# Block-wise turning of attention probabilities on VectorE with row-tiled context products, and a bitwise search for the top-k thresholds on ScalarE

## The chip, the core and the metric

The kernel runs on one core of one Trainium2 chip. The core has five instruction streams that run independently and meet through semaphores: TensorE (PE; its weight loads are shown apart as PEld), VectorE (DVE), ScalarE (ACT), GpSimd (POOL) and SyncE (SP), which issues most transfers. Each stream executes its instructions in the order in which the built program has them. The metric is device time of one execution in microseconds (us).

## What is computed

Four batches of 512 tokens with 512 features pass through two blocks. The parts that matter here:

```
# block 0, attention over contexts h (512 x 128 per batch)
sim       = einsum(Q, K) / (sqrt(32) * 4)             # 512 x 512
threshold = top_k(sim, 153)[..., -1:]                 # 153rd largest value of each row
A         = sigmoid(sim) * (sim >= threshold)
adj       = (A + A.T) * 0.5
x         = x + tanh(g) * ((1 - gamma) * layernorm(x) + gamma * adj)
# block 0, feed-forward: Hadamard rotations, 8-bit rows, ternary weights (feed0)
# block 1, attention with 16 heads over the rotated contexts kv_r (512 x 128)
scores    = einsum(q_r, k_r)                          # 16 heads, 512 x 512
attn      = softmax(scores)
ctx_c     = attn @ kv_r                               # per head, 512 x 128
x         = x + tanh(g) * (ctx_c projected by each head's 128 x 512 matrix, summed)
# block 1, feed-forward with normalized rows and ternary weights (feed1)
```

All products of the two attentions are in float32.

## The kernel before

**Order of the work.** Batch 0 passes alone through block 0 (`adjacency(0)`, `feed0(0)`), while `ahead` prepares what all batches need: the rotated contexts `kv`, one 128 x 512 output matrix per head (`om`, kept in DRAM), and the keys. Then `attention` (L917) walks through 4 x 8 pairs of heads. Each pair has four steps, one for each 128 rows j of queries. In a step `scores(j)` makes the score products of both heads, and the *next* pair's preparation is put in (`head`: query projections pqh; `rope`: products pb and rotation; `rotated`: product pr). After each step a planner (L1029) adds background work: `before(b)` for batches 1 to 3, which is the block-0 work of the next batch (`adjacency`, `keys`, `feed0`), and for the last batch `last_weights`, which makes block 1's ternary weights and runs `feed1` of batches 0 to 2. Each background generator yields a cost, and a job's costs (230 for a batch, 260 for the last) are spread over its steps. `feed1` of batch 3 ends the kernel. The framework places the instructions at build time in the streams of the engines, by priority and by its own estimate of when they are free; `tc.high_priority` moves instructions ahead, a negative offset moves them back.

**One pair of heads.** `scores(j)`: two products pss (L863, L866), each with 64 rows of the contraction in its own half of the array; VectorE finds the row maximum nm (L871), ACT makes the exponential pp with the row sum (L874) and scales it by the reciprocal (L877). `turn(j)` (L880), two steps behind the scores: TensorE transposes the four 128 x 128 blocks of pp through the identity into ppt (L885), ACT copies ppt to pT (L886). `attended` (L888), when all four tiles are turned: for each head four products of 128 contexts each accumulate pc (L893), and ACT copies it to cxo (L898). `added` (L901): four output products po of two heads each (L905), and VectorE adds them to the tokens x (L910). The heads' `om` are loaded at the start of the pair.

**The top-k threshold.** `adjacency(b)` (L447) takes two row tiles at a time. ACT copies the similarities to sim (L477). Twenty rounds follow: VectorE's MAX8 finds the eight largest of each row (L486), and MATCH_REPLACE overwrites them with a very low number (L491); the 153rd value falls out of the last round. These 20 rounds stand for each of the 16 row tiles of the four batches, put back in priority:

```
for r in range(rounds):
    with tc.high_priority(offset=-FILL):
        for j in pair:
            nc.vector.max(m8[j], cur[j])
    yield 1.3
    with tc.high_priority(offset=-FILL):
        if r < rounds - 1:
            for j in pair:
                nc.vector.match_replace(works[j], m8[j], cur[j], GONE)
    yield 1.4
```

Then a sigmoid on ACT (L496) and one VectorE operation (L497) make the masked values, and L512 to L524 symmetrize them and add them to x.

**Memory.** PSUM has eight banks: four for products (`ps`, tag mm), two for transposes (`pst`, tag tr) and two for background work (`psb`). pT has two buffers of 128 x 2048, one per head.

## Time and profile before

| | |
|---|---|
| three runs, median (lowest to highest) | 2048.83 us (2048.23 to 2052.68) |
| profiled execution, span | 2048.8 us |
| PE busy | 1819.6 us, 89% |
| DVE busy | 1630.3 us, 80% |
| ACT busy | 1081.8 us, 53% |
| POOL busy | 336.1 us, 16% |
| first and last score products (L863) start at | 286.3 and 1914.3 us |
| mean granted TensorE clock | 0.96 of full speed |

The profile is one execution. A line of the groups gives the source line, engine, operation, what is written and read, shapes and count; after the first bar the busy time of the group in us and the mean length of one in ns; after the second the idle time of the engine just before these instructions and what ended it. A float32 product appears as two passes in the counts of PE and PEld. A line of the timeline begins with start and length in us. A line of a stretch gives from, to and length, then for PE, PEld, DVE, ACT and POOL the busy us (and instructions), then the granted clock, the share of the DMA engines and GB/s.

### The profile page before, as it was taken

The page shows a single profiled execution, that of the slowest core. Times are in us where ns is not written, and L with a number is a line of the kernel's source. Part 1 is how long each engine was busy: PE and PEld are TensorE (multiplying, and loading weights), DVE is VectorE, ACT ScalarE, POOL GpSimd, SP SyncE. Part 2 cuts the span into 40 slices and gives each one's busy share as a digit, 9 for nine tenths or more (in the row PEclk, how much of TensorE's full clock was granted, in tenths as well). Part 3 has the DMA queues.
Part 4 walks back from the last instruction along what each step waited for, and adds up shares of the span by engine and source line. Part 5 has one row for each costly group of instructions (what it writes and reads, how often), then busy time and mean ns, then how long its engine had stood idle before and what let it go on. Part 6 is the DMA issues. An engine that isn't in the chain of part 4 may idle for free. (4 is left out here: it accounts for less than half of the span.)

```text
span 2048.8 us, 22947 instructions
## 1 busy us (share of the span) xinstructions
PE 1819.6 (89%) x7874; PEld 889.2 (43%) x7874; DVE 1630.3 (80%) x3305; ACT 1081.8 (53%) x1833; POOL 336.1 (16%) x316
## 2 busy tenths in 40 slices
PE   1268799999999999999999999999989999999898
PEld 0035534436554344455444444555443444444333
DVE  7989699987776999977778999778758556866785
ACT  6935454354434455453444564534786565555544
POOL 3020031123011122130111221301111210111000
PEclk6579899999999999999999999999999999999999
DMA  7451021111111222111122121111783112222011
GB/s 269 155 179 38 1 74 45 55 49 28 42 43 48 89 71 72 38 38 37 41 55 84 57 84 47 35 35 38 241 302 128 50 40 74 68 53 67 21 34 39
DMA packets 115556, 151.90 MB, mean 74 GB/s; under 512 B 57456, under 2 KB 68080, under 8 KB 112368
## 3 DMA queue, kind: packets, MB, share of 16 engines
q1 hardware_dynamic: 109968, 134.51, 22.0%
q0 software_dynamic: 4320, 14.16, 1.9%
q10 hardware_dynamic: 1152, 1.77, 0.2%
q8 instruction: 62, 1.02, 0.2%
q14 instruction: 54, 0.44, 0.1%
HBM read 117.90 MB, written 19.92 MB: 67 GB/s over the span
## 5 line engine op out<-in xcount | busy, mean ns | idle before, releaser
L833 POOL TENSOR_TENSOR ro<-ro,rs 128x512 f32<-128x512 f32 x192 | 255.4, 1333 | 1153.3 <-DVE rs L829 648.3
L874 ACT ACTIVATE pp<-pss,nm 128x512 f32<-128x512 f32 x256 | 174.6, 685 | 272.3 <-DVE nm L871 271.5
L804 PE MATMUL pqh<-hT,wq 128*128 128x512 f32 x512 | 239.7, 606 | 6.8 <-ACT pp L874 5.6
L893 PE MATMUL pc<-pT,kv 128*128 128x512 f32 x512 | 236.0, 600 | 2.7 <-ACT pT L886 2.6
L905 PE MATMUL po<-om,cxo 128*128 128x512 f32 x512 | 229.9, 597 | 0.0
L819 PE MATMUL pb<-qh,wc 128*128 128x512 f32 x384 | 189.4, 613 | 13.6 <-ACT qh L809 7.7
L486 DVE MAX8 m<-work 128x8 f32<-128x512 f32 x304 | 198.7, 684 | 0.6
L871 DVE TENSOR_REDUCE nm<-pss 128x1 f32<-128x512 f32 x256 | 167.8, 683 | 38.1 <-PE pss L866 37.9
L491 DVE MATCH_REPLACE8 work<-m,work 128x512 f32<-128x512 f32 x288 | 193.6, 678 | 0.1
L877 ACT ACTIVATE pp<-pp,rsm 128x512 f32<-128x512 f32 x256 | 178.6, 720 | 27.4 <-DVE rsm L876 26.2
L886 ACT COPY pT<-ppt 128x512 f32<-128x512 f32 x256 | 142.1, 588 | 38.5 <-PE ppt L885 38.0
L885 PEld LDWEIGHTS ppt<-ident,pp 128*128 128x128 f32 x1024 | 117.7, 142 | 96.6 <-issue 37.1
L885 PE MATMUL ppt<-ident,pp 128*128 128x128 f32 x1024 | 147.8, 279 | 10.1 <-ACT pp L877 4.4
L910 DVE SCALAR_TENSOR_TENSOR x<-po,gt,x 128x512 f32<-128x512 f32 x128 | 94.8, 745 | 68.4 <-PE po L905 67.6
L804 PEld LDWEIGHTS pqh<-hT,wq 128*128 128x128 f32 x512 | 93.1, 191 | 128.4 <-issue 89.6
L863 PE MATMUL pss<-kr,qr 64*128 64x512 f32 x256 | 143.4, 641 | 4.4 <-ACT pp L874 2.6
L905 PEld LDWEIGHTS po<-om,cxo 128*128 128x128 f32 x512 | 93.9, 190 | 119.5 <-issue 101.2
L866 PE MATMUL pss<-kr,qr 64*128 64x512 f32 x256 | 143.4, 641 | 0.7 <-DVE ro L827 0.5
L827 DVE TENSOR_TENSOR ro<-pb,cos_q 128x512 f32<-128x512 f32 x192 | 130.9, 682 | 10.3 <-PE pb L819 9.5
L893 PEld LDWEIGHTS pc<-pT,kv 128*128 128x128 f32 x512 | 91.9, 190 | 105.0 <-issue 90.4
L819 PEld LDWEIGHTS pb<-qh,wc 128*128 128x128 f32 x384 | 65.6, 189 | 113.6 <-issue 40.9
L898 ACT COPY cxo<-pc 128x512 f32<-128x512 f32 x64 | 37.4, 584 | 145.1 <-PE pc L893 144.8
(279 smaller groups left out, 3062.0 us busy)
## 6 DMA issues: line engine op xcount, KB each, us to landing
wq<-in_wqh SPq DMA_DIRECT2D x64, 256.0 KB, 2.7
om<-omd SPq DMA_DIRECT2D x64, 256.0 KB, 2.8
wc<-in_wkcq SPq DMA_DIRECT2D x32, 384.0 KB, 3.1
krd<-krs POOLq DMA_DIRECT2D x32, 256.0 KB, 2.5
kr<-krd SPq DMA_DIRECT2D x32, 256.0 KB, 2.7
sa_w1v<-in_gvT SPq DMA_DIRECT2D x8, 1024.0 KB, 5.3
sb_w1v<-in_gvT SPq DMA_DIRECT2D x8, 1024.0 KB, 5.2
wr<-in_wqr SPq DMA_DIRECT2D x32, 192.0 KB, 2.4
```

The costliest lines, as they stand in the source:

```text
L486: nc.vector.max(m8[j], cur[j])
L491: nc.vector.match_replace(works[j], m8[j], cur[j], GONE)
L804: nc.tensor.matmul(pq, self.wqs[i][:, c, :], hT[self.b][:, c, :], start=(c == 0), stop=(c == NC - 1),)
L819: nc.tensor.matmul(pb, self.wc[:, at : at + P], self.qhs[i if i < 2 else o], start=True, stop=True)
L833: nc.gpsimd.tensor_tensor(ro, ro, rs, ALU.add)
L863: nc.tensor.matmul(*args, start=True, stop=True)
L871: nc.vector.tensor_reduce(nm, pss[i], AX.X, ALU.max, negate=True)
L874: nc.scalar.activation(pp, pss[i], AF.Exp, bias=nm, accum_out=sm)
L877: nc.scalar.activation(pp, pp, AF.Copy, scale=rs)
L885: nc.tensor.transpose(pt[:, l, :], pp[:, l * P : (l + 1) * P], ident)
L893: nc.tensor.matmul(pc, kv[self.b][:, l, :], self.pT[i][:, l, :], start=(l == 0), stop=(l == NT - 1),)
L905: nc.tensor.matmul(po, self.cxo[i][:, j * P : (j + 1) * P], self.oms[i], start=(i == 0), stop=(i == 1),)
```

## The change

There are two changes, and what follows from them.

1. **Turning and context product.** `turn(j)` no longer uses TensorE and ACT: VectorE transposes each 128 x 512 tile of probabilities in blocks of 32 x 32, and writes pT. What was at (row 32a + r, context 32c + s) is then at partition 32a + s, column 32c + r: the contexts of one block lie over 32 partitions, and the four groups of 32 partitions hold the four groups of query rows. So `attended` makes 64 products per pair, each with 32 rows of contraction, for context block c and row group g: 32 contexts (kvrep, partitions 32g to 32g + 31) times 256 query rows of both heads. The four groups accumulate in four banks, and ACT copies four pieces to cxo. The contexts have to lie in each of the four groups, so `kvrep` (8 KB per partition) is loaded four times from DRAM for each batch, by `values(b)`; `ahead` writes the rotated contexts to DRAM, and `keys` reads them back. A pair's context and output products now come in the first step of the next pair, behind its first scores and the next query projection. `turn(j)` comes in the step of its scores. The heads' `om` are loaded in that first step as well, behind the previous pair's output products. pT has one buffer for both heads.
2. **Thresholds of batches 1 to 3.** Instead of 20 rounds on VectorE a search finds the threshold bit by bit for all four row tiles at once: ACT counts with Sign and its accumulator how many values of a row lie above a test value (four passes over 128 x 512), and VectorE sets or clears a bit by three operations on 128 x 4. One count for the sign and 31 for the bits follow each other; each needs the previous one's result. Batch 0 keeps the rounds. The tokens x are loaded behind the search.
3. PSUM: the two transpose banks join the products' (six of one kind). The scratch tiles for the start (cxo, pT) are taken from other rings.

The core of the diff:

```diff
-    ps = ctx.enter_context(tc.tile_pool(name="ps", bufs=4, space=bass.MemoryType.PSUM))
-    pst = ctx.enter_context(tc.tile_pool(name="pst", bufs=2, space=bass.MemoryType.PSUM))
+    ps = ctx.enter_context(tc.tile_pool(name="ps", bufs=6, space=bass.MemoryType.PSUM))
...
+    def kth(b, sims):
+        st = small.tile([P, 8, NT], F32, tag="kth", name=f"kth_{b}", bufs=1)
+        cnt, sig, need, test, r, u, hi, lo = (st[:, k, :] for k in range(8))
+        ints = lambda t: t.bitcast(I32)
+        junk = gate_t(f"signs_{b}")
+
+        def signs(**how):
+            for j in range(NT):
+                col = slice(j, j + 1)
+                nc.scalar.activation(
+                    junk, sims[:, j, :], AF.Sign, accum_out=cnt[:, col],
+                    **{k: v[:, col] for k, v in how.items()},
+                )
...
+        for bit in range(30, -1, -1):
+            signs(scale=sig, bias=test)
+            nc.vector.tensor_tensor(ints(r), cnt, need, ALU.is_lt)
+            if bit:
+                nc.vector.tensor_scalar(
+                    ints(r), ints(r), bit, 1 << (bit - 1), ALU.logical_shift_left, ALU.bitwise_or
+                )
+            nc.vector.tensor_tensor(ints(test), ints(test), ints(r), ALU.bitwise_xor)
+            yield 3.4
...
+        for j in range(NT):
+            nc.vector.tensor_scalar(
+                junk, sims[:, j, :], hi[:, j : j + 1], 0.0, ALU.is_ge, ALU.add,
+                accum_out=cnt[:, j : j + 1],
+            )
+        nc.vector.tensor_scalar(ints(u), cnt, float(TOPK), None, ALU.is_ge)
+        nc.vector.copy_predicated(lo, ints(u), hi)
+        yield 5.0
+        return lo
...
+        if not alone[0]:
+            for j in range(NT):
+                psim = bg_ps(f"psim_{b}_{j}")
+                nc.tensor.matmul(psim, qT[:, j * P : (j + 1) * P], kT, start=True, stop=True)
+                nc.scalar.activation(adj[:, j, :], psim, AF.Copy, scale=SIM_SCALE)
+                yield 1.0
+            limit = yield from kth(b, adj)
+            tokens()
+            for j in range(NT):
+                sg = front_t(f"sig_{b}_{j}")
+                nc.scalar.activation(sg, adj[:, j, :], AF.Sigmoid)
+                nc.vector.scalar_tensor_tensor(
+                    adj[:, j, :], adj[:, j, :], limit[:, j : j + 1], sg, ALU.is_ge, ALU.mult
+                )
+        for two in range(0, NT if alone[0] else 0, 2):
...
+    def values(b):
+        t = const.tile([P, 16, DC], F32, tag="kvrep", name=f"kvrep_{b}")
+        rows = kv_d[b].rearrange("(a i) j d -> i j a d", i=32)
+        for g in range(4):
+            nc.sync.dma_start(
+                t[32 * g : 32 * g + 32].rearrange("i (j a) d -> i j a d", j=NT), rows
+            )
+        kv[b] = t
...
         def turn(self, j):
+            if self.pT is None:
+                self.pT = wp.tile([P, 2, NT, S], F32, tag="pT", name=f"pT_{self.u}", bufs=1)
             for i in range(2):
-                pt = tr_ps(f"ppt_{self.u}_{i}_{j}")
-                pp = self.pps.pop((i, j))
-                for l in range(NT):
-                    nc.tensor.transpose(pt[:, l, :], pp[:, l * P : (l + 1) * P], ident)
-                nc.scalar.copy(self.pT[i][:, :, j * P : (j + 1) * P], pt)
+                nc.vector.transpose(self.pT[:, i, j, :], self.pps.pop((i, j)))
 
         def attended(self):
-            self.cxo = []
-            for i in range(2):
-                pc = mm_ps(f"pc_{self.u}_{i}")
-                for l in range(NT):
-                    nc.tensor.matmul(
-                        pc, kv[self.b][:, l, :], self.pT[i][:, l, :],
-                        start=(l == 0), stop=(l == NT - 1),
-                    )
-                cxo = wp.tile([P, S], F32, tag="cxo", name=f"cxo_{self.u}_{i}", bufs=3)
-                nc.scalar.copy(cxo, pc)
-                self.cxo.append(cxo)
+            pcs = [mm_ps(f"pc_{self.u}_{g}") for g in range(4)]
+            for c in range(16):
+                for g in range(4):
+                    rows = slice(32 * g, 32 * g + 32)
+                    with tc.high_priority() if c + g else nullcontext():
+                        nc.tensor.matmul(
+                            pcs[g][:, : 8 * 32], kv[self.b][rows, c, :],
+                            self.pT[rows, :, :, 32 * c : 32 * c + 32].rearrange("p i j s -> p (i j) s"),
+                            start=(c == 0), stop=(c == 15), skip_group_check=True,
+                        )
+            self.cxo = wp.tile([P, 8, 4, 32], F32, tag="cxo2", name=f"cxo_{self.u}", bufs=1)
+            for g in range(4):
+                nc.scalar.copy(self.cxo[:, :, g, :], pcs[g][:, : 8 * 32].rearrange("p (m s) -> p m s", m=8))
...
         for at, (b, g) in enumerate(order):
             nxt = begin(*order[at + 1]) if at + 1 < len(order) else None
-            cur.oms = out_weights(b, g)
             for j in range(NT):
                 cur.scores(j)
...
-                if j > 1:
-                    cur.turn(j - 2)
+                if j == 0:
+                    if prev:
+                        ended(prev)
+                    cur.oms = out_weights(b, g)
+                cur.turn(j)
                 yield b, g
-            cur.turn(NT - 2)
-            cur.turn(NT - 1)
             if nxt:
                 nxt.rotated()
-            cur.attended()
-            cur.added()
```

`ended(p)` is `p.attended()`, `p.added()` and, for the last pair of a batch, the spills of x that stood at the end of the loop, then `values(b + 1)`.

## The prediction

> **What bounds the kernel now.** I read the page's busy table first (PE 89%, DVE 80%, ACT 53%), then busy time by stretches between score products of chosen pairs, then the costliest groups, last single stretches of the timeline. The stretches (us; PE, PEld, DVE, ACT, POOL busy; clock, DMA share, GB/s):
>
> ```profile
> 286.00:406.00 120.00, 115.19 (x362) 48.99 (x362) 117.67 (x262) 56.35 (x116) 23.42 (x19) 1.00 0.16 48
> 406.00:655.00 249.00, 232.83 (x1277) 126.86 (x1276) 195.26 (x352) 114.19 (x210) 43.88 (x42) 0.99 0.17 44
> 655.00:789.00 134.00, 127.95 (x403) 55.35 (x402) 123.31 (x279) 68.02 (x134) 25.61 (x23) 1.00 0.23 71
> ...
> 1485.00:1907.00 422.00, 399.31 (x1399) 175.31 (x1400) 280.91 (x548) 253.80 (x407) 63.14 (x48) 0.99 0.32 95
> ```
>
> From the first score product (286.3) to the last (1914) TensorE is busy about 95% of every stretch: it sets the length. ACT has more than half of each stretch free. The price rows:
>
> ```profile
> L486 DVE MAX8 m<-work 128x8 f32<-128x512 f32 x304 | 198.7, 684 | 0.6
> L893 PE MATMUL pc<-pT,kv 128*128 128x512 f32 x512 | 236.0, 600 | 2.7 <-ACT pT L886 2.6
> ...
> L491 DVE MATCH_REPLACE8 work<-m,work 128x512 f32<-128x512 f32 x288 | 193.6, 678 | 0.1
> ...
> L886 ACT COPY pT<-ppt 128x512 f32<-128x512 f32 x256 | 142.1, 588 | 38.5 <-PE ppt L885 38.0
> ...
> L885 PE MATMUL ppt<-ident,pp 128*128 128x128 f32 x1024 | 147.8, 279 | 10.1 <-ACT pp L877 4.4
> ```
>
> Two heads' scores, the one pair of row tiles in the kernel (start, duration):
>
> ```profile
> 1619.29 0.69 PE L863 MATMUL pss<-kr,qr 64*128 64x512 f32 x1
> ...
> 1619.30 0.69 PE L866 MATMUL pss<-kr,qr 64*128 64x512 f32 x1
> ...
> 1619.83 0.59 PE L863 MATMUL pss<-kr,qr 64*128 64x512 f32 x1
> 1619.83 0.59 PE L866 MATMUL pss<-kr,qr 64*128 64x512 f32 x1
> ```
>
> The two tiles run side by side, pass by pass. And ACT early in the kernel: an accumulating pass that must wait for the previous one, then a pass with per-row scale and bias:
>
> ```profile
> 29.56 1.89 ACT L239 ACTIVATE ja_w0g<-sa_w0g 128x2048 bf16<-128x2048 f32 x1
> 31.36 0.18 ACT L239 ACTIVATION_READ_ACCUMULATOR ja_w0g<-sa_w0g 128x1 f32 x1
> 31.58 1.91 ACT L239 ACTIVATE ja_w0u<-sa_w0u 128x2048 bf16<-128x2048 f32 x1
> ...
> 51.38 0.19 ACT L239 ACTIVATION_READ_ACCUMULATOR ja_w0u<-sa_w0u 128x1 f32 x1
> 51.48 0.80 ACT L514 ACTIVATE x<-x,ckm,ckr 128x512 f32<-128x512 f32 x1
> 52.18 1.90 ACT L239 ACTIVATE ja_w0u<-sa_w0u 128x2048 bf16<-128x2048 f32 x1
> ```
>
> **The change, engine by engine.** The sum goes against the profiled execution: its span of 2048.8 is the median of the three runs (2048.83) to 0.03 us, so I use one number for both.
>
> *TensorE, transposes.* 1024 transposes go. In the timeline eight take 0.87 to 1.04 us from start to start of what follows, so 0.12 each: -120 us, 3.7 per pair of heads (the 147.8 busy counts overlapping tails).
>
> *TensorE, context.* Now a pair takes 7.06 us (16 passes of 0.43). After, 64 products of 256 columns, two passes of half of 0.43 each: 0.43 us a product. Four tiles side by side give 16 x 0.43 = 6.9, all in line 27.5. Two row tiles side by side are in the trace, four are not; I take 6.9 and keep 27.5. But the tiles are not dealt evenly: in the built program's order 12 of the 32 pairs begin like 0,1,0,2,1,3,2,1,3,2 and leave 8 to 14 products of one tile for the end, which nothing accompanies. Walking each pair's order with 0.43 per product and in-order start gives 301 us against 32 x 7.06 = 226: +75. TensorE nets -120 + 75 = -45 us.
>
> The Trainium skill, "TensorE: Matmul & The Clock Gate", section "Part 3: Packing small matmuls", speaks against a full factor of four: it gives 3.07 for four row tiles. By it an even pair would take 27.5 / 3.07 = 9.0 us, an estimate, and the 23 pairs outside the searches would add some 23 x 2 = 47 us to the sum below; no run here shows that figure.
>
> *VectorE.* Gone: 240 MAX8 (0.68), 228 MATCH_REPLACE (0.68) with their loads (0.08): 337 us. New: 256 block transposes; no such row; nearest are 128x512 passes from 0.54 (L184) up to 1.22 for a 1024 wide one (L588); I take 0.68: 174. Some 320 operations on 128x4 at 0.16 to 0.25: 65; twelve 128x512 counts: 8. Net -90, and it stays below TensorE in each stage. The transposes of tile 0 stand in VectorE's line behind the previous pair's context product, as pT has one buffer: VectorE idles there for the product (7 to 12 us). In pairs where it has 50 to 57 us of work beside TensorE's 53 to 57 that shows; I put 8 us per non-search stage.
>
> *ACT.* Gone: 256 copies of 0.59 (142 us). New: 384 counts (3 batches x 32 x 4). Scale and bias by row make 0.80 long, 0.70 start to start (L514 above, against 0.62 for the plain L496); the accumulator read adds 0.10. All counts write one scratch tile, so each waits for the one before: above, a pass into the same scratch starts 0.22 after the accumulator read (31.36 to 31.58), one that is free of it 0.10 after (51.38 to 51.48): +0.12. That is 0.80 without and 0.92 with the wait; lower bound 0.68, the exponential's step. I take 0.90: 346 us. Between bits ACT needs three dependent VectorE operations (0.24 each where such a chain stands, as 229.91, 230.15 at L192 and L194) and two hand-overs of under 0.1: 0.85. In the built order a bit's first count follows the last bit's count directly 59 times.
>
> *Where these counts stand.* This decides. They are not spread over a batch: 109 of batch 1's lie in pairs 0 to 2, all 128 of batch 2's in the first three pairs of their stage, batch 3 the same, most of them in a pair's first step. A typical first step on ACT: two exponentials, two scalings, qh, 18 counts, context copy, count, two copies, 6 counts, copy, 9 counts: 3.2 + 34 x 0.9 + 4 x 0.35 + 8 x 0.85 = 42 us. TensorE's part of that step is 1.1 + 3.6 + 7 to 12 + 7 = 19 to 24 us, and its output product, then the next scores, stand behind the four copies, so behind 25 counts. TensorE waits.
>
> ACT per search stage, from its busy time in the stretch. Batch 1 (286 to 406): 56.4 - 14.1 (24 copies) + 0.7 (context in four pieces) + 98 + 14 (bit waits) = 155, TensorE 103. Batches 2 and 3 (655 to 789, 1069 to 1203): 68 - 14.1 + 0.7 + 115 + 17 + 8 (six more table loads of 1.28) + 3 (two sigmoids, four yb copies moved in) = 198, TensorE 139.
>
> *Elsewhere* TensorE decides. I sum its row prices pair by pair. A plain pair before: pqh 7.3, pb 5.7, pss 4.2, pr 2.7, ppt 3.7, pc 7.1, po 7.0, in all 37.7; the trace has 39.9 from scores to scores, and over all pairs a factor of 1.065 (small waits) gives 1623 for the 1628 us between first and last scores. After, with the uneven tiles, TensorE comes to 218, 260, 260 and 428 in the four stages outside the searches. Stages, before and after: pairs 0 to 2, 120 and 155; 3 to 6, 249 and 228; 7 to 9, 134 and 198; 10 to 14, 280 and 268; 15 to 17, 134 and 198; 18 to 22, 282 and 268; 23 to 31, 428 and 440 (uneven tiles eat the transposes' gain there, and pair 23 has 60 us of ACT work, most of it weight passes ahead of its context copies, against TensorE's 51). Sum 1628 and 1755: +127.
>
> *Costed at nothing.* kvrep, four loads of 256 KB a batch on SP's queue behind the spills and ahead of om: the 256 KB wq lands in 2.7 us, and its first use is a pair (40 us) later; without that cover some 10 us a batch. The context and output products of a pair, with their spills, now follow the next pair's first scores, and om's loads follow them on SP's queue; om is used a pair later. kvd and kvl: one round trip per batch, with pairs to spare. Larger rings for oms and krs at the start: at most the 10 us that pO waits for oms, taken as 0.
>
> Forecast 2048.8 + 127 = **2175 us**.
>
> **Rivals.**
> 1. *ACT keeps up, TensorE decides (faster).* Place: the three search stages. For it: ACT is half idle there (56 of 120). They would take TensorE's 103, 139 and 139, with the others at their sums without my 8s: 1560, so 1985 us. The point: outside the searches I expect -36, so they may take 388 + 36 = 424 us; ACT's other work there is 57 + 83 + 83 = 223; 365 counts must fit in 201, 0.55 us each. Rows say 0.80 at least, and no row with an accumulator is under 0.68.
> 2. *Four tiles do not run side by side (much slower).* 27.5 instead of 7 to 13 per pair: the searches mostly hide it under ACT, the other pairs add about 19 each: some 2600. Against: the L863 and L866 starts, 10 ns apart.
> 3. *The searches cost as said, but less:* counts at 0.80 and bit waits hidden behind exponentials: 25 to 30 less per search stage, and no 8s: 2065. It has my forecast's mechanism at its lower bounds; upper bounds, transposes at 1.22 in VectorE's fullest pairs (+30), uneven tiles and a clock that drops while TensorE waits (0.62 in 0 to 100 us, +25), end at 2255.
>
> **How the numbers follow.** Searches bound by ACT (forecast with rival 3's lower end): 0.78, nearly all of it slower, 2045 to 2260. TensorE decides: 0.15, 1985 to 2045. Tiles in line: 0.05. Unchanged by balance: 0.02. The range 2045 to 2260 leaves out most of the second and all of the third, 2 in 10. A measurement of this kernel tells about 0.2% (4 us) from no change: faster 0.14, same 0.03, slower 0.83.
>
> **What would show it.** Right: in the three search stages ACT busy over 80% and TensorE under 75%, its longest waits at po for cxo and at pss or pqh for the exponentials; counts 0.9 apart; four pc products starting within 0.1 us of each other, ends of some pairs with one tile alone for 3 to 6 us; other stages 10 to 20 us shorter. Wrong: counts under 0.6 apart; TensorE over 90% in the searches; pc taking over 20 us in each pair; VectorE the releaser TensorE waits for longest.

## The result and the profile after

The changed kernel takes 2491.9 us (median of four runs, 2488.1 to 2493.4) against 2050.8 us (2048.2 to 2053.5) for the kernel before in the same job: 1.215 times as long, 95% interval 1.213 to 1.217, so +441 us where +126 was forecast. The direction was right; the time lies above the range, whose upper end was 2260. The profiled execution has a span of 2491.6 us.

The engines' busy line and the row of granted clocks on the page of the changed kernel:

```profile
PE 1885.5 (76%) x10434; PEld 993.9 (40%) x10434; DVE 1563.8 (63%) x3213; ACT 1317.0 (53%) x2433; POOL 330.1 (13%) x320
...
PEclk6658997799998877999887788999877899999899
```

No engine is near full any more. TensorE's share falls from 89% to 76%: it stands still for 606 us (span less busy time) where it stood for 229. Its mean granted clock falls from 0.960 to 0.860. Next the stretches that answer to those of before (us; busy time of PE, PEld, DVE, ACT, POOL; clock, DMA share, GB/s): pairs 0 to 2, 3 to 6, 7 to 9, and 23 to the last score.

```profile
322.60:492.30 169.70, 113.69 (x458) 53.22 (x458) 78.55 (x203) 142.96 (x315) 22.81 (x18) 0.80 0.11 33
492.30:747.30 255.00, 219.42 (x1550) 129.16 (x1550) 191.63 (x350) 100.43 (x193) 43.62 (x43) 0.92 0.15 43
747.30:987.80 240.50, 154.34 (x692) 76.71 (x692) 105.58 (x283) 174.83 (x383) 25.47 (x23) 0.79 0.16 46
...
1839.50:2359.00 519.50, 440.39 (x2252) 215.12 (x2252) 339.02 (x672) 258.57 (x402) 62.85 (x48) 0.90 0.31 96
```

In the search stages ACT is busy 84%, then 73% (174.83 of 240.50), TensorE 67 and 64%: one waits for the other in turn. Where nothing is searched TensorE falls short as well, 86% and 85%, and those stretches were to become shorter.

Every stage (first score of a pair to first score of another; "head" is up to the first score), with four of the experiments told below; the forecast's stages stand beside, the last one as its 440 to the last scores and the 135 that follow them in before:

| us | before | forecast | after | e1 | e2 | e9 | e10 |
|---|---|---|---|---|---|---|---|
| head | 286.3 | 286 | 322.6 | 320.5 | 285.9 | 319.3 | 320.6 |
| pairs 0-2, search | 119.9 | 155 | 169.7 | 158.2 | 139.7 | 151.0 | 146.7 |
| 3-6 | 248.9 | 228 | 255.0 | 252.1 | 262.8 | 235.5 | 242.5 |
| 7-9, search | 134.1 | 198 | 240.5 | 204.9 | 149.3 | 215.2 | 170.8 |
| 10-14 | 280.1 | 268 | 305.5 | 287.3 | 293.9 | 285.7 | 274.0 |
| 15-17, search | 133.9 | 198 | 239.0 | 204.2 | 159.2 | 188.7 | 170.0 |
| 18-22 | 282.1 | 268 | 307.2 | 287.5 | 300.2 | 285.6 | 272.4 |
| 23 to the end | 563.5 | 575 | 652.1 | 643.7 | 577.0 | 616.5 | 581.6 |
| span | 2048.8 | 2175 | 2491.6 | 2358.4 | 2168.0 | 2297.5 | 2178.6 |

The stages are named after the changed kernel, whose counts end with pairs 2, 9 and 17 but for five in pair 3. In the other columns part of the search runs on into the stage that follows: in e2 pairs 7 to 11 hold 28, 29, 30, 27 and 14 of the counts on record, in the changed kernel pairs 7 to 9 hold 50, 40 and 38.

**What TensorE waits for.** From the waits of TensorE in the changed kernel (us in total, times, longest):

```profile
PE po L996 <- ACT cxo L989: 160.4, 17, 21.5
PE pr L882 <- POOL ro L925: 142.3, 37, 9.9
PE pd_f L439 <- DMA zT_f<-q_f: 41.5, 5, 10.6
```

The kernel before had no wait of po for the copies on its list, and of the other two

```profile
PE pr L790 <- POOL ro L833: 10.0, 13, 1.3
...
PE pd_f L436 <- DMA zT_f<-q_f: 6.5, 7, 1.5
```

The first was forecast, the other two were not. The third stands mostly where a batch's preparation ends. The first two can be seen in one search pair (pair 8, 68.9 us; before 42.4). ACT's rows in its first step:

```profile
862.80 0.81 ACT L464 ACTIVATE signs<-adj,kth 128x512 f32<-128x512 f32 x1
863.52 0.19 ACT L464 ACTIVATION_READ_ACCUMULATOR signs<-adj,kth 128x1 f32 x1
863.74 0.81 ACT L464 ACTIVATE signs<-adj,kth 128x512 f32<-128x512 f32 x1
864.46 0.18 ACT L464 ACTIVATION_READ_ACCUMULATOR signs<-adj,kth 128x1 f32 x1
865.33 0.81 ACT L464 ACTIVATE signs<-adj,kth 128x512 f32<-128x512 f32 x1 [0.69 <-DVE kth L482]
...
884.99 0.35 ACT L989 COPY cxo<-pc 128x256 f32<-128x256 f32 x1
```

A count starts 0.94 us after the one before it and 1.59 after a bit's last one, so a bit costs 4.41 us (4.45 by the forecast's 0.90 and 0.85). The fourth context copy stands behind all counts up to 884.99. TensorE in the same pair:

```profile
855.88 13.87 PE L982 MATMUL pc<-pT,kvrep 32*128 32x256 f32 x128
885.39 9.76 PE L996 MATMUL po<-om,cxo 128*128 128x512 f32 x16 [15.63 <-ACT cxo L989]
...
908.81 0.64 PE L882 MATMUL pr<-ro,wr 128*64 128x512 f32 x1
...
915.63 1.12 PE L882 MATMUL pr<-ro,wr 128*64 128x512 f32 x1 [5.75 <-POOL ro L925]
```

The context product was done at 869.7; po could start 15.6 us later and runs 9.76 us instead of the 7.1 that it took before (below). At the pair's end pr waits 5.75 us and its next pass takes 1.12 instead of 0.64. In the changed kernel's pair 26, after a shorter wait, it does not:

```profile
2079.59 0.64 PE L882 MATMUL pr<-ro,wr 128*64 128x512 f32 x1 [1.20 <-POOL ro L925]
```

How the pair's end looked before (pair 26, one with no search):

```profile
1641.07 0.64 PE L790 MATMUL pr<-ro,wr 128*64 128x512 f32 x1
...
1642.74 1.04 PE L885 MATMUL ppt<-ident,pp 128*128 128x128 f32 x8
1643.71 0.64 PE L790 MATMUL pr<-ro,wr 128*64 128x512 f32 x1
...
1644.72 7.13 PE L893 MATMUL pc<-pT,kv 128*128 128x512 f32 x16
1651.69 7.12 PE L905 MATMUL po<-om,cxo 128*128 128x512 f32 x16
```

Transposes lie between the parts of pr, and the last rotated tiles come in time. The context and output products follow the last part of pr here, so they covered nothing of that chain; they lie ahead of it in pairs with much other work (pair 5: 12 of 16 passes of pc).

The rows of what was added:

```profile
L464 ACT ACTIVATE signs<-adj,kth 128x512 f32<-128x512 f32 x372 | 302.0, 812 | 90.6 <-DVE kth L482 82.3
L982 PE MATMUL pc<-pT,kvrep 32*128 32x256 f32 x4096 | 307.2, 380 | 0.0
...
L974 DVE STREAM_TRANSPOSE pT<-pp 128x512 f32<-128x512 f32 x256 | 169.3, 691 | 125.0 <-PE pc L982 119.1
```

These sizes are close to the forecast's (0.80, 301 us, 0.68). What failed is not these prices but what TensorE waits for.

### The profile page after: what moved, and what is told of

Its sections match the earlier page's. It is cut to its first block, busy times and chain, and to the rows that moved or that the text cites. A ratio compares the mean times of both kernels' runs of the same rounds, so it can differ in the third digit from the quotient of the medians.

```text
span 2491.6 us, 28671 instructions
## 1 busy us (share of the span) xinstructions
PE 1885.5 (76%) x10434; PEld 993.9 (40%) x10434; DVE 1563.8 (63%) x3213; ACT 1317.0 (53%) x2433; POOL 330.1 (13%) x320
## 4 chain that ended last, share of the span: by engine, by line
PE 45%; DVE 25%; ACT 21%; DMA 4%; issue 3%; POOL 1%; SPq 0%; ACTq 0%; POOLq 0%; DVEq 0%
ACT signs L464 10%; PE po L996 10%; PE pqh L896 7%; PE pc L982 6%; PE pss L953 3%; DVE rs L924 3%; DVE nm L961 2%; PE pd_f L439 2%; DVE ro L919 2%; PE pzh_f L679 2%; ACT pp L964 2%; PE pb L911 2%; PE pr L882 2%; DVE pT L974 2%; PE pd_g L439 1%
## 5 line engine op out<-in xcount | busy, mean ns | idle before, releaser
L996 PE MATMUL po<-om,cxo 128*128 128x512 f32 x512 | 258.7, 661 | 160.5 <-ACT cxo L989 160.4
L464 ACT ACTIVATE signs<-adj,kth 128x512 f32<-128x512 f32 x372 | 302.0, 812 | 90.6 <-DVE kth L482 82.3
L982 PE MATMUL pc<-pT,kvrep 32*128 32x256 f32 x4096 | 307.2, 380 | 0.0
L982 PEld LDWEIGHTS pc<-pT,kvrep 32*128 32x128 f32 x4096 | 272.8, 185 | 42.5 <-issue 13.7
L896 PE MATMUL pqh<-hT,wq 128*128 128x512 f32 x512 | 257.2, 643 | 2.5 <-ACT hT L854 2.5
L974 DVE STREAM_TRANSPOSE pT<-pp 128x512 f32<-128x512 f32 x256 | 169.3, 691 | 125.0 <-PE pc L982 119.1
L882 PE MATMUL pr<-ro,wr 128*64 128x512 f32 x192 | 120.3, 731 | 142.6 <-POOL ro L925 142.3
L953 PE MATMUL pss<-kr,qr 64*128 64x512 f32 x256 | 162.3, 717 | 16.3 <-ACT qr L942 16.2
L956 PE MATMUL pss<-kr,qr 64*128 64x512 f32 x256 | 162.3, 718 | 0.0
L477 DVE TENSOR_TENSOR kth<-kth 128x4 int32<-128x4 f32 x93 | 17.1, 183 | 226.3 <-ACT signs L464 225.8
L884 PE MATMUL pr<-ro,wr 128*64 128x512 f32 x192 | 120.3, 731 | 0.0
L989 ACT COPY cxo<-pc 128x256 f32<-128x256 f32 x128 | 40.5, 375 | 139.7 <-PE pc L982 139.7
```

The lines of the kernel that those rows point to most:

```text
L464: nc.scalar.activation(junk, sims[:, j, :], AF.Sign, accum_out=cnt[:, col], **{k: v[:, col] for k, v in how.items()},)
L896: nc.tensor.matmul(pq, self.wqs[i][:, c, :], hT[self.b][:, c, :], start=(c == 0), stop=(c == NC - 1),)
L953: nc.tensor.matmul(*args, start=True, stop=True)
L974: nc.vector.transpose(self.pT[:, i, j, :], self.pps.pop((i, j)))
L982: nc.tensor.matmul(pcs[g][:, : 8 * 32], kv[self.b][rows, c, :], self.pT[rows, :, :, 32 * c : 32 * c + 32].rearrange("p i j s -> p (i j) s" ...
L996: nc.tensor.matmul(po, cxo[:, NT * i + j, :], self.oms[i], start=(i == 0), stop=(i == 1))
```

## The experiments

Times are medians; ratios are to the kernel before in the same job, with 95% intervals. The kernel before took 2048.6 to 2052.7 us in these jobs.

### The change in two halves: e1_rounds, e2_bits_only

e1 is the changed kernel with the adjacency function of the kernel before (rounds of maxima on VectorE for all batches). e2 is the kernel before with `kth` and the changed adjacency function, and nothing else.

> The changed kernel with the thresholds of batches 1 to 3 found by the rounds of maxima on VectorE again, as before; turning by VectorE, four row tiles and the new place of the context and output products stay. Theory 1 (two causes of like size: the counts hold ACT in the search stages, and the rotated queries are waited for in the last step of every pair because the previous pair's context and output products no longer cover that chain): the three search stages, 649 us in the changed kernel and 388 before, fall to some 420 to 450; the head (+36) and the waits of pr for the rotated tiles (142 us) stay; about 2270 us, 2220 to 2320. Rival (the counts carry nearly all of the +441): 2050 to 2100.

> The kernel before with the bit-by-bit search by ACT's counts in batches 1 to 3 and nothing else of the change. Theory 1: the search stages grow as ACT's line does, by about 190 of the 261 us that they grew in the changed kernel; the other stages and the head stay within 10 us of before; about 2240 us, 2180 to 2300. Rival (the counts carry nearly all): 2420 to 2500. If ACT keeps up (under 0.55 us per count), 2050 or less.

Measured: e1 2359.5 us (1.150, 1.148 to 1.152), e2 2165.0 us (1.055, 1.052 to 1.057). The counts alone cost 113 us, the rest of the change alone 308; the sum of 421 leaves 20 to their meeting. The rival falls twice. But theory 1 had both sizes wrong as well, and both times lie outside its ranges: the counts cost less than its 190 (60 us of the 113 in the search stages, the rest in the others), and the search stages of e1 (567 us, 388 before) did not come back to 420 to 450 without them. In e1 the wait of pr stays (139 us), and a new one stands beside it, pb for a PSUM bank that a late addition of x on VectorE holds, 73 us.

### The pair's own end again: e3_own_end

```
             if nxt:
                 nxt.rotated()
+            ended(cur)
             cur, prev = nxt, cur
-        ended(prev)
```

(The call in step 0 goes; `out_weights` moves back to the pair's start.)

> The changed kernel with one thing undone: a pair's context and output products stand at its own end again, behind the next pair's rotation products, and its output weights are loaded at its start. Theory 1 (uncovered chain of rotated tiles, 7 to 8 us in each of 31 pairs): the waits of pr for the rotated tiles fall from 142 us to below 30, the last 9 pairs' stage falls from 520 us to 430 or so, and the time to about 2290 us, 2230 to 2350. Rival (that wait is only where another shortage shows, such as VectorE's transposes or ACT): the wait moves to pc for pT, and the time stays within 2440 to 2510.

Measured: 2457.0 us (1.197, 1.195 to 1.199), 35 us less, and pr still waits 134 us for the rotated tiles, po 142 for the copies. The rival's range holds, though the wait does not move to pc. Theory 1 falls: with pc and po at the pair's own end again the wait of pr stays, so it was not they that had covered it. pc needs the last turn, and is issued behind pr, as in the kernel before. In pair 25 VectorE runs without a break from 1964.5 to 1975.0 us (multiplications of the second rotation, two turns, two maxima, six multiplications of the third rotation, two turns); the third rotation's last multiplication ends at 1973.8, and pr, which had nothing but other parts of pr and one small transpose beside it, gets its tile at 1975.23.

### Who makes pr wait: e6_rope_early, e7_cover, e8_turn_twice

e6: `nxt.rope(2)` directly behind `nxt.rope(1)` in step 2, none in step 3. e7: in `turn`, ahead of VectorE's transpose,

```
+                pt = tr_ps(f"ppt_{self.u}_{i}_{j}")
+                for l in range(NT):
+                    nc.tensor.transpose(pt[:, l, :], pp[:, l * P : (l + 1) * P], ident)
                 nc.vector.transpose(self.pT[:, i, j, :], pp)
```

e8: that `nc.vector.transpose` twice.

> The changed kernel with the next pair's third rotation (its two products, six VectorE multiplications, two GpSimd additions) issued a step earlier, with the second one. Theory 4 (in every pair TensorE stands at pr for the rotated tiles, since nothing of its own is left to do between the rotation's products and pr; each such stand also lowers the clock of what follows): the wait of pr for the rotated tiles falls from 142 us to below 50, and the time by 80 to 150, to 2340 to 2410. Rival (VectorE's burst of multiplications, maxima and turned tiles in these steps is the line that counts, so the wait only moves to the scores or the maxima): 2470 to 2500.

> The changed kernel with the 1024 transposes on TensorE put back beside VectorE's turning, into PSUM tiles that nobody reads: only their time on TensorE comes back (147 us of busy time before, some 120 in line). Theory 4 (TensorE has idle time where they stood, ahead of pr; what the change took from TensorE was cover, not time): the time stays within 2470 to 2520, the wait of pr for the rotated tiles falls to about 60 and the granted clock rises from 0.86. Rival (TensorE's line sets the length): 2590 to 2620.

> The changed kernel with each 128x512 block turning on VectorE done twice, 256 more of 0.69 us, 177 us of VectorE work. Theory 5 (the turns stand in VectorE's line ahead of the rotation's multiplications and of the maxima, in the steps where TensorE waits): +100 to +177, 2590 to 2670, the wait of pr for the rotated tiles over 180 us. Rival (VectorE, busy 63% of the span, takes them in its idle time): below 2530.

Measured: e6 2430.9 (1.185, 1.184 to 1.187), pr's wait 59.9 us: 61 us less, between the 80 expected and the rival's 22 at most. e7 2528.8 (1.233, 1.231 to 1.235): the 1024 transposes, counted as 120 us of TensorE in the forecast, cost 37. Its waits:

```profile
PE ppt L977 <- ACT pp L967: 67.8, 54, 4.5
...
PE pr L882 <- POOL ro L925: 19.5, 18, 2.4
```

Half of pr's wait turns into a wait of the transposes for the probabilities, the rest is filled, and the clock rises to 0.889. e8 2542.4 (1.240, 1.237 to 1.242): 177 us of VectorE work cost 50, and pr waits 172 us. The 50 us lie between theory 5 and its rival. So both theories hold in part: TensorE's transposes were cover (83 of the 120 us counted for them was no gain), and VectorE's turns stand in the line that pr waits for (28% of what is added to them shows).

### The uneven tiles: e5_even

```
-                    with tc.high_priority() if c + g else nullcontext():
-                        nc.tensor.matmul(
+                    with tc.high_priority() if c + g else nullcontext(), tc.issue_after(last.ins) if c + g else nullcontext():
+                        last = nc.tensor.matmul(
```

> The changed kernel with the 64 products of each pair issued in strict turn over the four row tiles. By in-order start and 0.43 us a product the order built then takes 219 us instead of 301 for all pairs. Theory 1: outside the search stages (23 of 32 pairs) TensorE still has these products in its line, so about 55 us come off: 2437 us, 2410 to 2465; pc's first start to last end 6.8 to 7.7 us in every pair. Rival (the uneven ends lie in time that TensorE waits for the rotated tiles or ACT anyway): within 12 us of 2492.

Measured: 2476.6 (1.207, 1.205 to 1.209): 15 us less, not 55. pc's busy time falls from 307 to 231 us, but the wait of po for the copies rises from 160 to 212: most of the uneven ends lay beside ACT's counts. The rival is nearer. A pair's 64 products take 7.19 us in strict turn in 31 of 32 pairs of e5. In line they would take 64 x 0.43 = 27.5, an estimate from the ends of the changed kernel's pairs, where one tile is alone and its passes start 0.21 to 0.22 us apart (pair 8), two to a product. That makes 3.8 times as fast.

### The products' place: e9_split_even, e10_split_rounds_even

```
                 cur.scores(j)
+                if prev and j == 0:
+                    prev.attended()
+                    if prev.g == NG - 1 and prev.b < B - 1:
+                        values(prev.b + 1)
                 if nxt:
...
-                if j == 0:
+                if j == NT - 1:
                     if prev:
                         ended(prev)
```

(`ended` then holds `added` and the spills only.) e9 has e5's even order too, e10 also e1's rounds.

> The changed kernel with the even order of the row tiles, and with a pair's two products parted: the context product directly behind the next pair's first scores and ahead of its first query product, the output product with om's loads in the next pair's last step, between the third rotation and pr. No work is taken out; the context copies on ACT have three steps to land before po, and po stands where TensorE waited for the rotated tiles. Theory 6 (what was lost is cover: the place of pc and po made TensorE wait for ACT's copies at po, for the rotated tiles at pr, and for the next batch's normalised rows at the batch changes): po's wait for cxo falls from 212 to below 60 us, pr's from 143 to below 40, the pairs 7, 15 and 23 (102, 99 and 101 us in the changed kernel) to 60 to 85, and the time from 2476.6 to 2180 to 2330. Rival (ACT's counts in the search stages and VectorE's line hold TensorE wherever the products stand): above 2400.

> The same with the thresholds of batches 1 to 3 found by the rounds on VectorE, as before: turning by VectorE in 32x32 blocks, even row tiles, parted products, old search. Theory 6: 2359.5 less some 15 (even order), 130 (pr) and 70 (batch changes): 2140, 2060 to 2200. Rival (VectorE, with turns and rounds, is the line that counts in the search stages): 2250 to 2340.

Measured: e9 2300.3 (1.121, 1.119 to 1.123), e10 2179.6 (1.063, 1.061 to 1.065). Nothing is taken out, and e9 is 176 us under e5 (98 of them in the search stages), e10 180 under e1 (e5's even order in it). TensorE's waits in e9:

```profile
PE pss L956 <- ACT cxo L989: 168.9, 10, 19.6
...
PE pr L882 <- POOL ro L925: 10.4, 9, 6.9
```

pr's wait is nearly gone, as the output product lies ahead of it. The wait for the copies is not gone: it moved from po to the scores of the next step, whose banks pc still holds. Nor did the batch changes come to the 60 to 85 us of theory 6: pairs 7, 15 and 23 take 95, 67 and 95 us (in e10, without counts, 51, 51 and 64). The plainest pair, 26, takes 34.9 us in e9, 39.5 before, 43.4 in the changed kernel: there the turning and the row tiles do seem to pay, some 4 us. But its other work is not quite the same (12 background transposes before, 8 in e9; 4 and 16 feed-forward products in the changed kernel), and pairs 24 to 26 together take 124.5 us in e9, 121.2 before.

### The head: e4_head_even, e11_split_rounds_head

```
+        if alone[0]:
+            return ps.tile([P, 512], F32, tag="mm", name=name)
+        ring[0] = (ring[0] + 1) % 6
+        if ring[0] < 4:
+            return ps.tile([P, 512], F32, tag="mm", name=name)
+        return pst.tile([P, 4, P], F32, tag="tr", name=name).rearrange("p c q -> p (c q)")
```

(with `ps` of four banks and `pst` of two, and turned tiles from `pst` while `alone[0]` holds.) e4 has e5's even order, e11 is e10 with this.

> The changed kernel with the even order of the four row tiles, and with PSUM in the head dealt as before (a ring of four for products and one of two for turned tiles until the first scores of the loop; from there the six banks go round in one line, as in the change). Theory 3 (the one ring of six queues the first gate products behind the turned tiles of all four row blocks): the first scores come at 286 to 292 us instead of 322.6 and the time is 30 to 37 us under that of the even order alone (2476.6), 2440 to 2447. Rival (the head is late by the round trip of the context rows and by the rings of the stored products): first scores still at 315 to 323 us, time 2470 to 2480.

> The same as the one before it, with PSUM dealt as a ring of four and a ring of two until the loop's first scores. Theory 3 for the head: first scores at 286 to 292 us and 30 us less in all: 2110, 2030 to 2170; if it comes under 2049 the turning and the row tiles pay once they are placed. Rival: the head's gain is given back in the first pairs, as with the even order alone (2479 against 2477): within 10 us of the one before.

Measured: e4 2479.3 (1.209, 1.206 to 1.211), first scores at 290.3 us; e11 2192.0 (1.070, 1.067 to 1.073), first scores at 288.7. Theory 3 is right on the head, and the rival on the time: the 32 us are given back by later stages in e4 (3 us over e5, no more than the jobs differ) and in e11 (12 over e10). What the one ring did in the changed kernel's head, on TensorE:

```profile
157.55 1.12 PE L635 MATMUL pn_f<-ident,n_f 128*128 128x128 f32 x4 [5.74 <-DVE n_f L632]
...
164.37 0.61 PE L210 MATMUL ptq_af<-identb,qa_f 128*128 128x128 bf16 x4 [2.96 <-ACT qa_f L216]
...
171.57 1.11 PE L635 MATMUL pn_f<-ident,n_f 128*128 128x128 f32 x4 [5.74 <-DVE n_f L632]
```

Row block after row block, 14 us each, with no gate product between. In e4 the first gate product starts at 153.06, behind the first block; in the changed kernel at 192.9, behind the fourth.

### The order of the background: e12 to e15

```
-                    spent += next(gen)
+                    with ExitStack() as behind:
+                        for ins in tail.values():
+                            behind.enter_context(tc.issue_after(ins.ins))
+                        spent += next(gen)
```

(`tail` holds the step's last turn on VectorE, and ACT's last scaling and last context copy.) e12 is e10 with it, e13 is e9, e14 the changed kernel, e15 e11.

> The kernel of e10 (old search by rounds, even tiles, parted products) with one line of order added: each piece of the background work that is drawn after a step is queued on VectorE behind that step's turn and on ACT behind its last scaling and the last context copy. Theory 7 (order, not load): the search stages fall from 147, 171 and 170 us to 120 to 140 each, the 19 us waits of the scores for the probabilities' banks go, and the time falls from 2179.6 to 2050 to 2120. Rival (VectorE's load, 98% in these stages): the rounds only move into the next stages, 2160 to 2210.

> The kernel of e9 (search by ACT's counts, even tiles, parted products) with the same line of order. Theory 7: no block of up to 25 counts ahead of the context copies any more; search stages from 151, 215 and 189 us to 130 to 160, time from 2300 to 2130 to 2220. Rival (ACT's load of counts): 2270 to 2320.

> The changed kernel with that line of order alone: products unparted, tiles uneven. Theory 7 with theory 6: po's wait for the context copies falls from 160 to below 80 us, pr's for the rotated tiles stays at 120 to 145; 2492 to 2370 to 2440. Rival: 2470 to 2510.

> The kernel of e12 with PSUM in the head dealt as a ring of four and one of two. Theory 3: first scores at 286 to 292 us and, where nothing behind gives it back, 30 us under e12: 2020 to 2090, so perhaps under the kernel before. Rival: within 12 us of e12, the head's gain given back in the first pairs.

What led to it, in pair 8 of e10: TensorE's third scores (the second head's two passes in one row)

```profile
798.84 2.07 PE L938 MATMUL pss<-kr,qr 64*128 64x512 f32 x2 [19.05 <-ACT pp L946]
```

wait while VectorE, from 765.4 to 793.0 us, does nothing but MAX8 and MATCH_REPLACE8 for the search; the pair's turn of tile 0, which needs pc (over at 768.7), comes behind them at 793.0.

Measured: e12 2224.5 (1.084, 1.082 to 1.086), 45 us more than e10; e13 2245.9 (1.094, 1.093 to 1.096), 54 less than e9; e14 2469.0 (1.202, 1.200 to 1.205), 23 less than the changed kernel; e15 2217.7 (1.081, 1.079 to 1.083), 7 less than e12 with the first scores at 284.2. None of the four times comes into its theory's range. With counts the order matters: in e14 po's wait for the copies falls from 160 to 31.6 us, pr's stays (159). But only 23 us come of 129: the time comes back elsewhere, in the stages without search (pairs 3-6 from 255 to 273, 10-14 from 306 to 329). With rounds theory 7 fell: e12's search stages are 139, 168 and 162 us, hardly under e10's 147, 171 and 170, and pairs 10-14 and 18-22 grow by 27 and 25 as the rounds slip into them (40 MAX8 on record in pairs 10 to 12, 15 in e10). That fits the rival, VectorE's load: in e10 it is busy 116.9 of the 118.5 us of pairs 1 and 2.

### Batch changes and spreading: e16 to e18

e16 is e13 with `b * per - 2 * NT` for `b * per - NT` in the jobs; e17 adds `yield 6.0` for `yield 3.4` and 313.2 for 230.0; e18 adds the head's two rings.

> The kernel of e13 (counts, even tiles, parted products, background queued behind each step) with the background of each batch due one pair earlier, eight steps ahead of the batch's end instead of four. Theory 8 (at a batch change the drained end of the next batch's preparation is a chain of short waits that nothing covers since pc and po stand behind it): the pairs 7, 15 and 23 (113, 66 and about 95 us) fall to 45 to 65 each, the two before them grow by some 10; 2246 to 2150 to 2200. Rival (the chain costs the same wherever it is drained): 2230 to 2260.

> The kernel of e16 with the 31 bits drawn more slowly: 6.0 instead of 3.4 units of background a bit, and the batch's total raised by the same 83, so that the counts lie over some 14 to 18 steps instead of 12. Theory 7 for the counts (their place, not their sum): the steps of 18 to 27 us in the search pairs fall to 8 to 15, and the time by another 20 to 60 under e16. Rival (the sum of counts on ACT, 115 us a batch, or the rest of the preparation pressed into fewer steps): the same as e16 or up to 40 us more.

> The kernel of e17 with PSUM in the head dealt as a ring of four and one of two. Theory 3: first scores 25 to 32 us earlier than in e17, and 15 to 35 us off the time, between 2070 and 2150. Rival: within 12 us of e17, given back in the first batch, as in e4, e11 and e15.

What led to it, on TensorE in the first step of pair 7 of e13:

```profile
737.67 5.56 PE L439 MATMUL pd_f<-wd_w,zT_f 128*128 128x512 fp8e4 x16 [15.15 <-DMA zT_f<-q_f]
743.08 4.01 PE L679 MATMUL pzh_f<-had_sb,ya_f 128*128 128x128 f32 x32
757.68 5.80 PE L439 MATMUL pd_f<-wd_w,zT_f 128*128 128x512 fp8e4 x16 [10.59 <-DMA zT_f<-q_f]
```

The forced end of the next batch's preparation is a chain, and nothing of the loop lies beside it; before, pair 6's context products and the first of its output products lay between pzh_f and the last pd_f of that chain.

Measured: e16 2240.7 (1.094, 1.092 to 1.095), e17 2223.9 (1.085, 1.083 to 1.087), e18 2217.3 (1.082, 1.080 to 1.084). Theory 8 names the place rightly: pairs 7, 15 and 23 take 57.6, 56.3 and 46.5 us in e16, 112.8, 65.5 and 67.9 in e13 (the 95 in the expectation is e9's pair 23). But pair 3 grows from 58 to 77 and pairs 8 and 9 from 50 and 49 to 61 each, and 5 us are left of it, no more than the jobs differ: the rival is right on the time. e17's 17 us are just under the 20 expected. e18's first scores come 27 us earlier, its end 7, as its rival said.

No version here beats the kernel before. The nearest, e10, is 127 us over it (2179.6 against 2052.7). By the stages of the two profiled executions: head +34, the three search stages +27, +37 and +36, the others -6, -6 and -10, pair 23 to the end +18.

## Why the prediction was wrong

**The step that failed** is "*Elsewhere* TensorE decides. I sum its row prices pair by pair", with the 1024 transposes as a saving of 120 us in that sum. In the four stages outside the searches TensorE's busy time came close to the sum (1183 us, part of it at a lower clock, against 218 + 260 + 260 + 428 = 1166). But it stood still there for 204 us, where it had stood 72 before and the forecast left 38 above its sum. The largest part, 96 us, is pr's wait for the rotated tiles. The transposes had stood between the parts of pr, beside the rotation's way over VectorE and GpSimd: put back, they cost 37 us and pr's wait falls from 142 to 19.5 (e7). The turns that replace them lengthen that way: 256 more of them raise pr's wait to 172 us (e8).

The move "costed at nothing" failed as well: "The context and output products of a pair, with their spills, now follow the next pair's first scores". Undone as it stands it is worth only 35 us, and pr's wait stays at 134 (e3). What the place of these 14 us a pair can be worth is shown by e9 and e10: with the output product ahead of pr, and no work taken out, 176 us (e9 against e5) and 180 (e10 against e1, even order in it). So their old place had hardly covered pr; a new one can. At the batch changes they had covered something, the end of the preparation: pd_f's wait rose from 6.5 to 41.5 us. The forecast counted each engine's work and asked which sum was largest; it never asked what TensorE would do while it waited. The prediction's own section on costs at nothing named a pair's time for om, not what the products and transposes had covered.

**TensorE, transposes: -120.** By e7 they were worth 37: the rest of their time became waiting. **Context +75.** Size right (307 us busy against 301), effect 15 (e5), as the uneven ends lie beside waits.

**ACT.** The prices were nearly right (0.94 a count and 4.41 us a bit, for 0.90 and 4.45), and so was the first step of a search pair: 42 us forecast, 45.5 in pair 8. But the stage was taken as ACT's sum without a gap: 198 us, measured 240.5 with ACT busy 174.8, so that the "ACT over 80%" of the prediction's list holds in the first search stage alone (84, 73 and 73%). In pair 8's other three steps (23.3 us) it is VectorE that is busy, 21.2 us; ACT waits 4.9 us for the search's operations on it, and TensorE 5.75 for pr. The counts alone, in the old loop, cost 113 us (e2), 60 of them in these stages, where the forecast had +163. There they lie thinner, over four to five pairs, and po never waits for the context copies. Taken out of the new loop the same counts give back 132 (e1).

**VectorE -90.** Measured -67 (1630.3 to 1563.8), and 0.691 a turn. That it "stays below TensorE" is right for each stage's sum; it does not follow that nobody waits for it: pr's wait grows with VectorE's line (e8) and falls when the last rotation is issued a step earlier (e6).

**Elsewhere TensorE decides.** Forecast 228, 268, 268 and 440 (pair 23 to the last scores), measured 255, 306, 307 and 520: 184 of the 317 us that the forecast fell short. The search stages give 98, the head 36.

**"Larger rings ... taken as 0".** The head is 36 us longer. The merged PSUM ring, which the prediction did not price, is 32 of them: it puts the gate products behind four row blocks (first scores at 322.4 us in e5, 290.3 in e4). The 4 us left are all that the rings of oms and krs and the contexts' round trip can have cost; no run has them alone. What the PSUM ring costs in the end is open: each repair was mostly given back.

**Rivals.** Rival 1 (ACT keeps up) and rival 2 (tiles in line) are ruled out by 0.94 us a count and by 7.19 us a pair. The second had cited the Trainium skill, "TensorE: Matmul & The Clock Gate", "Part 3: Packing small matmuls", for a factor of 3.07 with four row tiles, there of 512 columns; for these products of 256 columns the runs give 3.8 (27.5 over 7.19), so the measurement decides against the 9.0 us a pair worked out from it.

**Sums.** Four of the prediction's readings do not hold, and none of them decides: ACT has less than half free in two of the four stretches shown (68.0 of 134 and 253.8 of 422 us busy); the stages outside the searches hold 10 and 12 us, not 8, where they go from 218 to 228 and from 428 to 440; rival 1's 1560 gives 1981 with the 421 us outside the loop, not 1985; and its upper bounds add up to 2230, not 2255, unless uneven tiles and clock bring 25 us each.

**The clock.** +25 at most was put into the range. po alone rises from 229.9 to 258.7 us, the query product from 239.7 to 257.2, the two heads' scores from 143.4 to 162.3 and pr from 99 to 120, the last two each counted once for two that run side by side: 86 us on the same work. It follows the long waits: 0.64 a pass after the 1.20 us wait at 2079.59, 1.12 after 5.75 us at 915.63. It also fell with no wait at all, at an uneven end: in pair 8 TensorE is busy without a break, but from 867.0 us its one tile's passes start 0.43 us apart instead of 0.22, and the granted clock is 1.00, 0.71 and 0.50 in the stretches from 864, 866 and 868 us, 1.9 us each. Pair 9's end, as uneven, kept the clock; no run tells why. The Trainium skill, "TensorE: Matmul & The Clock Gate", "Part 1: The HAM clock gate", says that the clock halves after at least one idle window of some 3.4 us and comes back after at least one busy one. The two waits agree. After the 15.6 us wait of pair 8 the passes of po are 0.85 us apart for 5.3 us, then 0.43, which is more than one such window.

What stays open: how e10's 34 us in the head and 18 behind pair 23 would be had without a loss elsewhere; and why the built order puts up to 25 counts ahead of the context copies here, and not in e2. That the build takes the row tiles' 64 products for longer than the 7 us that they need is a possible reason, which no run tests. In these runs nearly every gain at one place was partly given back at another, and no run tells which order has none.

## What to carry to other kernels

When an edit takes work out of a loop or moves it, list what waited beside it at the old place, and price each of those chains as if nothing covered it; a saving on an engine that then waits is worth only what is left (37 of 120 us here). Where the engine that is longest changes from step to step, as in pair 8, expect a stage to cost the sum of the steps' longest lines, not the largest of the engines' totals. Rings of buffers that are merged put unrelated work into one line: look for what is queued behind the slowest user.

## What the runs showed of the hardware

Four row tiles of 32 rows run nearly fully side by side: 64 products of 256 columns in 7.19 us, 3.8 times as fast as the 27.5 us estimated in line (from 0.215 a pass where one tile is alone). VectorE turns a 128x512 tile in 32x32 blocks in 0.691 us, where MAX8 over the same size takes 0.684 (before). A wait of 5.75 us nearly doubles the next pass (0.64 to 1.12 us), one of 1.20 us does not. The clock can also halve while TensorE is busy, with one row tile of 32 rows alone (pair 8: granted clock 0.50 from 868.0 to 869.9 us), though it did not at every such end.
